# Graph attention over 2708 nodes: five moves in the order of the work (M's block sums, additions of h, sort, W_v's differences, table entries)

## The chip, the cores and the metric

The kernel runs on one core of a Trainium2 chip. A core has TensorE (PE, matrix products; PEld is its loading of weights), VectorE (DVE), ScalarE (ACT), GpSimd (POOL) and SyncE (SP). DMAs are issued from the queues of SP, ACT and POOL. The metric is device microseconds (us) of one execution, as a median of several runs; one execution is also recorded by the profiler, and its trace is what the views below come from.

## The reference

One layer of masked attention over a graph, with a layer norm ahead, in float32. There are N = 2708 nodes of D = 1024 features; the adjacency matrix `adj` holds ones with a chance of 0.00148 each, so about four in a row.

```python
h = jnp.maximum(_layernorm(x, axis=-1), 0.0)
q = h @ W_q.T + b_q
k = h @ W_k.T + b_k
v = h @ W_v.T + b_v
z = scale * (q @ k.T)
spare_z = z * adj
spare_z = jnp.where(spare_z == 0.0, -10000.0, spare_z)
attn = softmax(spare_z, axis=1)
x = x + relu(attn @ v)
```

## The kernel before

**What it computes instead.** It never forms the 2708 x 2708 scores. W_q and W_k are multiplied into one matrix M (1024 x 1024), so that a score is the product of a row of h M + b with a neighbour's row of h. The sum over neighbours is taken over rows of h, and W_v is applied once to the result. Only the neighbours' rows are gathered.

**Rows and tiles.** Nodes stand in 22 tiles (21 of 128 rows and one of 20). Tiles 0 to 11 (`EARLY` = 12) are the early part, the others the late part; each part is sorted by degree, so that all rows of a sorted tile t have at most K[t] neighbours.

**The stages.**

1. *M* (lines 340 to 486, PE's `ps_x`, `ps_y`, `ps_z`). M is formed in four blocks by seven block products, each a sum over `term` calls. `joined` adds a bank into M on DVE. Beside it the statistics of x (`stats`, `root`, `apply`), the stores of h (`keep`) and the searches of adj (`edges`) run, in an order written out as text: `follow("e7 e8")` searches tiles 7 and 8; the letters are s (statistics), m (moments), r (root), a (apply), h (keep), e (edges).
2. *Queries* (units "q"). A unit is a pair of tiles. Its 256 x 1024 by 1024 x 1024 product is done with seven block products (`multiply`, PE's `ps` and `psy`), which need sums of M's blocks (`ts_of_m`, tile T, in `wlow`) and sums of the rows' blocks (`blocks`: `s1` to `s4`). ACT and DVE take the results (`c11`, `c12`, `c21`, `c22`). Units 0 to 5 (`FIRST` = 6) are tiles 0 to 11 in their natural order; later units work on sorted tiles, whose rows are gathered. The searches go on beside units 0 to 2 (`steps_at`).
3. *Sort* (`sort`, line 533). Counts and ranks by two products on PE (`ps_in`, `ps_all`, from `hot`), then the place of each node (`pos_i`). `put` stores the entries of the table (18 words for each node: neighbours, node number, degree) into DRAM at these places by indirect DMAs from POOL, and loads them back sorted (`ptab`).
4. *Attention* (`attention`, `scores`, `weights`, `sums`), a generator that DVE works through: for each sorted tile and slot a neighbour's rows (g) are gathered, multiplied with the query rows (pq, gathered for early tiles, loaded for late ones), exponentiated, and summed into u. `advance` takes steps of it between the products of units from `FIRST` on, `share` of time for each product.
5. *Outputs* (units "o"): pairs of u, again by seven products with W_v, whose blocks' differences (`ts_of_wv`) were stored to `tv_dram`; then x is added and the rows are scattered to the output. The last tile is done alone.

**What sets the order.** PE, SP and, after a point, the rest are ordered by a scheduler. In the stages up to the sort ACT, DVE and POOL run in the order of the program text (`manual_schedule`: `ordered` for ACT and DVE, `pooled` for POOL, closed in `after` at (3, 2)); DVE is in the order of the text again from unit 6 on. `tc.issue_after` holds an instruction behind another in the order of issue. In `after(i)`, line 1068, n is the unit and i the product behind which a step stands. Each engine works its queue in order, so a wait at its head holds all that stand behind it.

**The places the change touches.** `keep` (248): for each tile, a store of h from POOL's queue and an addition into `hsum` on POOL. The order of e7, e8 and the sums `ts_of_m(0, 0)` and `ts_of_m(1, 0, 1, 2, 3)` on DVE, and the product of the bias (`ps_v`, 479), whose halves are subtracted on DVE (483). The loads of W_k's first 128 rows from ACT's queue (348). `put` (511) and the end of `sort` (570). `ts_of_wv` (659): 16 subtractions and 16 stores. `after` (1068): where sort, the differences and the first step of `advance` stand. The index `half_i` (1147) is computed on DVE from the late part of the sorted table.

Of the kernel before, what the change touches and what calls it, by code (L numbers as in the profile page):

```python
# [18 lines left out]
P = 128  # L19
NB = 512  # L20
# [10 lines left out]
EARLY = 12  # L31
# [26 lines left out]
def tile_preln_masked_attention(  # L58
# [12 lines left out]
    nc = tc.nc  # L71
    N, D = x.shape
# [4 lines left out]
    NT = len(tiles)  # L77
# [10 lines left out]
    wk_rows = wk.rearrange("o p c w -> o (p c w)")  # L88
# [29 lines left out]
    hsum = const.tile([P, D], FT, name="hsum")  # L118
# [36 lines left out]
    t = 0  # L155
    while t < NT:
# [4 lines left out]
        t = e  # L161
# [83 lines left out]
                n = tiles[group[i]][1]  # L245
                nc.scalar.activation(xs[i][:n], xs[i][:n], AF.Relu, bias=r[:n, 4, i:i + 1], scale=r[:n, 3, i:i + 1])

    def keep(first):

        group, xs, r = normed.pop(first)  # L250
        for t, xt in zip(group, xs):
            t0, n = tiles[t]
            nc.gpsimd.dma_start(h_dram[t0:t0 + n, :], xt[:n])
            nc.gpsimd.tensor_add(hsum[:n], hsum[:n], xt[:n])  # L254

    normed, adj_loads, kept = {}, [], {}

    def follow(steps):

        for step in steps.split():  # L260
            first, *only = step[1:].split(".")
            first, *last = first.split("-")
            first = int(first)
            if step[0] == "s":
                stats(range(first, int(last[0]) + 1))
            elif step[0] == "m":
                moments(first)
            elif step[0] == "r":
                root(first)
            elif step[0] == "a":  # L270
                apply(first, *[range(int(o[0]), int(o[-1]) + 1) for o in only])
            elif step[0] == "h":
                keep(first)
            else:
                adj_loads.append(edges(first))

# [55 lines left out]
    def ts_of_m(part, *which):  # L332
        cut = slice(part * (P // NH), (part + 1) * (P // NH))
        m = [[M[:, i, j].rearrange("p c (b w) -> p (c b) w", w=P)[:, :, cut] for j in range(2)] for i in range(2)]
        t = [T[:, k].rearrange("p c (b w) -> p (c b) w", w=P)[:, :, cut] for k in range(4)]
        for k in which:
            a, b = ((m[0][1], m[0][0]), (m[1][1], t[0]), (m[1][1], m[0][1]), (m[1][0], t[1]))[k]
            nc.vector.tensor_sub(t[k], a, b)

    with tc.tile_pool(name="w", bufs=1, side="left") as wp:  # L340
# [3 lines left out]
        wk_sb = [wlow[:, H + o] for o in range(H)] + [wp.tile([P, D], FT, name=f"wk{o}") for o in range(H, DC)]  # L344
        for o in range(DC):
            nc.sync.dma_start(wq_sb[o], wq_rows[o * P:(o + 1) * P, :])
            for part in (slice(0, NB), slice(NB, D)) if o == 0 else (slice(0, D),):
                (nc.scalar if o < 2 else nc.sync).dma_start(wk_sb[o][:, part], wk_rows[o * P:(o + 1) * P, part])

        t1 = [work.tile([P, D], FT, tag="hT", name=f"t1_{k}", bufs=2) for k in range(2)]  # L350

# [109 lines left out]
        for i in range(H):  # L461
            term(Y[i], i, (0, 1), lambda o: b_half(o, 1))
            joined(Y[i], 1, 1, i)
            if i == 1:
                follow("a20 e4 a0 m2 m3")
        follow("e5 r2 h20 h0")
        for i in range(H):
            term(Z[i], i, (1, 0), lambda o: b_half(o + H, 1))
            joined(Z[i], 0, 1, i)
            if i == 0:  # L470
                follow("a2 e6")
        follow("e7 e8")
        ts_of_m(0, 0)
        ts_of_m(1, 0, 1, 2, 3)
        for i in range(H):
            if i == 2:
                for half in range(NH):
                    ps = psum.tile([P, NB], FT, tag="acc", name="ps_v")
                    nc.tensor.matmul(ps, ones, acc_b[:, half * NB:(half + 1) * NB], start=True, stop=True)
                    pw = P // NH  # L480
                    nc.scalar.copy(bp_sb.rearrange("q (c p) -> q c p", c=DC)[:, :, half * pw:(half + 1) * pw],
                                   ps.rearrange("q (p c) -> q c p", c=DC))
                nc.vector.tensor_sub(bp_sb[:, NB:], bp_sb[:, NB:], bp_sb[:, :NB])
            term(Y[i], i, (1, 1), lambda o: b_half(o + H, 0))
            evicted(Y[i], 1, 0, i)
# [13 lines left out]
    FIRST = EARLY // 2  # L499

    def first_rows(n):

        rows_of[FIRST + n] = [row_tile(f"qr_{t}") for t in (EARLY + 2 * n, EARLY + 2 * n + 1)]
        for k, row in enumerate(rows_of[FIRST + n]):
            last = gather(row, h_dram[:, :], EARLY + 2 * n + k, SLOTS, P)
        return last
# [1 line left out]
    def tiles_of(lo, hi):  # L508
        return list(enumerate(tiles))[lo:hi]

    def put(lo, hi):

        puts = []
        for t, (t0, n) in tiles_of(lo, hi):
            put = nc.gpsimd.indirect_dma_start(  # L515
                out=tab_dram[:, :], out_offset=bass.IndirectOffsetOnAxis(ap=pos_i[:n, t:t + 1], axis=0),
                in_=tab[:n, t, :], in_offset=None)
            for other in puts:
                tc.declare_no_dep(put.ins, other.ins, reason="rows of a permutation")
            puts.append(put)  # L520
        full = min(hi, FULL)
        loads = [nc.gpsimd.dma_start(ptab[:, lo:full, :],
                                     tab_dram[lo * P:full * P, :].rearrange("(t p) w -> p t w", p=P))]
        if hi > FULL:
            loads.append(nc.gpsimd.dma_start(ptab[:REST, FULL, :], tab_dram[FULL * P:, :]))
        for load in loads:
            for put in puts:
                tc.add_manual_dep(load.ins, put.ins.name,
                                  mybir.DependencyInfo(mybir.DependencyClass.Sync, mybir.DependencyReason.DATA),
                                  reason="every row of the part")  # L530
        return loads[-1]

    def sort():
# [33 lines left out]
                                    AX.X, ALU.add)  # L567
        placed = nc.vector.tensor_copy(pos_i, deg)

        put(EARLY, NT)  # L570
        with tc.issue_after(first_rows(0).ins):
            loaded = put(0, EARLY)
        with tc.issue_after(loaded.ins):
            first_rows(1)
        return placed

# [41 lines left out]
    def natural_rows(n):  # L618
# [5 lines left out]
    ops_of[0][2]()  # L624
    banks_of = {0: banks_for(bp_sb)}
    ts_of_m(0, 1, 3, 2)
    follow("h2")
    natural_rows(1)
    ps = psum.tile([P, NB], FT, tag="tp", name="ps_b")
    nc.tensor.matmul(ps[:, 0:3], ones, part, start=True, stop=True)  # L630
# [3 lines left out]
    nc.vector.tensor_scalar(large[:, 0:1], large[:, 0:1], 10000.0, None, op0=ALU.is_gt)  # L634
    nc.vector.tensor_scalar(large[:, 1:2], large[:, 1:2], 250000.0 / D, None, op0=ALU.is_gt)

    steps_at = {(0, 0): "s4-5 e9", (0, 1): "r4 e10", (0, 3): "e11 a4", (0, 5): "h4 s6-7 e12", (0, 6): "r6 e13",
                (1, 0): "a6 h6", (1, 1): "e14", (1, 3): "s8-9", (1, 5): "r8 e15", (1, 6): "e16 a8 h8",
                (2, 0): "s10-11", (2, 1): "e17 r10", (2, 3): "e18", (2, 5): "a10 h10 e19", (2, 6): "e20 e21"}

# [15 lines left out]
        assert len(adj_loads) == NT  # L656
        free.extend(slots + [M.rearrange("p i j (a c) w -> p i j a (c w)", a=2)[:, 0, 1, a, :] for a in range(2)])

    def ts_of_wv():
        with tc.issue_after(placed[0].ins):  # L660
            for c in range(4):
                b11, b12 = slots[2 * c][:, :NB], slots[2 * c][:, NB:]
                b22, b21 = slots[2 * c + 1][:, :NB], slots[2 * c + 1][:, NB:]
                nc.vector.tensor_sub(b11, b12, b11)
                nc.vector.tensor_sub(b12, b22, b12)
                nc.vector.tensor_sub(b22, b22, b11)
                nc.vector.tensor_sub(b21, b21, b22)
                for k, r in enumerate((b11, b22, b12, b21)):
                    nc.sync.dma_start(tv_dram[k][:, c, :], r)
# [387 lines left out]
    for n, unit in enumerate(units):  # L1057
# [8 lines left out]
        results = (q_results if kind == "q" else o_results)(ta, tb)  # L1066

        def after(i):
            if (n, i) == (3, 2):
                pooled.close()  # L1070
                with tc.issue_after(products[-1].ins):
                    placed.append(sort())
                ordered.close()
                ts_of_wv()
            if n == FIRST - 1 and i == 5:

                chain.append(behind[-1])
                next(stream)
            if n == FIRST - 1 and i == 6:
                chain.append(behind[-1])  # L1080
            if (n, i) >= (FIRST, 0):
                advance(share)
            if nxt is not None:

# [272 lines left out]
```

## Time and profile before

| | us |
|---|---|
| median of 3 runs (lowest, highest) | 680.77 (679.22, 680.97) |
| the profiled execution | 680.76 |
| its span, first to last instruction | 679.0 |
| PE, DVE, POOL, ACT busy | 655.5, 525.7, 410.6, 263.5 |
| mean granted clock of PE | 0.994 |
| DMA | 190.62 MB, mean 281 GB/s |

The span is 1.76 us shorter than the profiled execution's time. A row of the timeline has the start in us, the duration in us, the engine, the line of the kernel, the operation, output<-inputs, the shape, the count, and in brackets the idle time of the engine ahead of it with what ended it. A wait "A <- B: total, times, longest" says that A waited for B. Several instructions of one kind are merged in one row ("x2"); a "product" of a block on PE is 8 rows' worth (four matmuls in float32, two instructions each). Durations of PE are modelled at their ends.

### The profile page before, as it was taken

The page shows a single profiled execution, that of the slowest core. Times are in us where ns is not written, and L with a number is a line of the kernel's source. Part 1 is how long each engine was busy: PE and PEld are TensorE (multiplying, and loading weights), DVE is VectorE, ACT ScalarE, POOL GpSimd, SP SyncE. Part 2 cuts the span into 40 slices and gives each one's busy share as a digit, 9 for nine tenths or more (in the row PEclk, how much of TensorE's full clock was granted, in tenths as well). Part 3 has the DMA queues.
Part 4 walks back from the last instruction along what each step waited for, and adds up shares of the span by engine and source line. Part 5 has one row for each costly group of instructions (what it writes and reads, how often), then busy time and mean ns, then how long its engine had stood idle before and what let it go on. Part 6 is the DMA issues. An engine that isn't in the chain of part 4 may idle for free.

```text
span 679.0 us, 6344 instructions
## 1 busy us (share of the span) xinstructions
PE 655.5 (97%) x1764; PEld 332.9 (49%) x1764; DVE 525.7 (77%) x1002; ACT 263.5 (39%) x396; POOL 410.6 (60%) x396
## 2 busy tenths in 40 slices
PE   7999997999998999999999999999999999999995
PEld 4777764444444444434444444444444444444442
DVE  5999859997798422099989859898999989989301
ACT  3466965755762212123322212233432333322220
POOL 2549995166453666476765437676776787883342
PEclk9999999999999999999999999999999999999998
DMA  8997889598767934789997999989998889696653
GB/s 342 408 357 248 317 299 407 198 322 344 284 225 237 297 104 127 256 273 367 370 334 263 411 417 401 295 235 313 279 286 266 256 267 338 187 263 217 152 151 120
DMA packets 61588, 190.62 MB, mean 281 GB/s; under 512 B 9753, under 2 KB 10105, under 8 KB 60650
## 3 DMA queue, kind: packets, MB, share of 16 engines
q0 software_dynamic: 34176, 107.67, 48.9%
q1 hardware_dynamic: 26362, 79.32, 31.7%
q10 hardware_dynamic: 1008, 3.15, 1.3%
q8 instruction: 16, 0.26, 0.2%
q14 instruction: 26, 0.21, 0.1%
HBM read 159.81 MB, written 43.88 MB: 300 GB/s over the span
## 4 chain that ended last, share of the span: by engine, by line
PE 52%; DVE 16%; issue 12%; DMA 10%; POOL 5%; ACT 2%; POOLq 0%; ACTq 0%; DVEq 0%
PE ps L840 19%; PE psy L840 14%; PE ps_y L368 6%; DVE u L777 5%; PE ps_x L368 5%; PE ps_z L368 4%; DMA u_dram<-u 3%; DVE junk L724 3%; DMA y<-in_x_dram,tab 3%; POOL g L494 2%; PE pt L311 2%; PE lone_q L1033 2%; DVE s L590 2%; DMA g<-h_dram,tab 2%; DVE at L292 2%
## 5 line engine op out<-in xcount | busy, mean ns | idle before, releaser
L494 POOL DMA_INDIRECT g<-h_dram,tab x107 | 133.1, 1244 | 62.7 <-issue 23.0
L840 PE MATMUL ps<-M,a 128*128 128x512 f32 x320 | 144.3, 593 | 0.1
L840 PE MATMUL psy<-wlow,s 128*128 128x512 f32 x320 | 144.1, 592 | 0.0
L724 DVE SCALAR_TENSOR_TENSOR junk<-g,pq 128x1024 uint8<-128x1024 f32 x95 | 116.3, 1224 | 22.7 <-DMA pq<-q_dram,tab 15.5
L777 DVE SCALAR_TENSOR_TENSOR u<-g,coef,u 128x1024 f32<-128x1024 f32 x78 | 100.1, 1283 | 7.4 <-ACT u L769 4.3
L840 PEld LDWEIGHTS ps<-M,a 128*128 128x128 f32 x320 | 59.4, 190 | 68.2 <-issue 67.4
L840 PEld LDWEIGHTS psy<-wlow,s 128*128 128x128 f32 x320 | 59.2, 190 | 66.5 <-issue 66.5
L840 PE MATMUL psy<-wlow,a 128*128 128x512 f32 x160 | 72.6, 596 | 5.7 <-DVE q L906 3.6
L840 PE MATMUL ps<-wlow,s 128*128 128x512 f32 x160 | 73.7, 604 | 3.5 <-ACT part L631 3.5
L292 DVE FIND_INDEX8 at<-ones,adj 128x8 uint32<-128x685 f32 (+1 forms) x88 | 74.4, 865 | 0.0
L840 PE MATMUL ps<-M,s 128*128 128x512 f32 x160 | 72.1, 592 | 0.0
L930 POOL DMA_INDIRECT y<-in_x_dram,tab x21 | 36.9, 1755 | 36.4 <-DMA tail_dram<-y 11.4
L285 ACT ACTIVATE sized<-adj 128x2708 uint8<-128x2708 f32 (+1 forms) x22 | 54.2, 2465 | 6.5 <-DMA adj<-in_adj_dram 5.4
L254 POOL TENSOR_TENSOR hsum<-hsum,x 128x1024 f32<-128x1024 f32 (+1 forms) x22 | 52.5, 2387 | 0.5
L840 PEld LDWEIGHTS psy<-wlow,a 128*128 128x128 f32 x160 | 29.8, 190 | 45.5 <-issue 34.4
L840 PEld LDWEIGHTS ps<-wlow,s 128*128 128x128 f32 x160 | 30.9, 194 | 43.2 <-issue 38.3
L840 PEld LDWEIGHTS ps<-M,s 128*128 128x128 f32 x160 | 30.2, 190 | 36.8 <-issue 36.4
L590 DVE TENSOR_TENSOR s<-a,pt 128x512 f32<-128x512 f32 x40 | 25.7, 681 | 15.2 <-ACT a L586 15.2
L769 ACT ACTIVATE u<-g,coef 128x1024 f32<-128x1024 f32 x16 | 18.4, 1149 | 46.6 <-DVE coef L768 46.6
L586 ACT COPY a<-pt 128x512 f32<-128x512 f32 x60 | 33.1, 591 | 7.3 <-PE pt L311 7.3
L678 POOL DMA_INDIRECT out_dram<-y,tab x21 | 30.3, 1442 | 8.9 <-issue 5.8
L515 POOL DMA_INDIRECT tab_dram<-tab,pos_i x22 | 24.1, 1094 | 8.3 <-issue 6.1
(234 smaller groups left out, 864.0 us busy)
## 6 DMA issues: line engine op xcount, KB each, us to landing
adj<-in_adj_dram SPq DMA_DIRECT2D x21, 1354.0 KB, 12.0
x<-in_x_dram SPq DMA_DIRECT2D x21, 512.0 KB, 10.9
h_dram<-x POOLq DMA_DIRECT2D x21, 512.0 KB, 6.3
u_dram<-u POOLq DMA_DIRECT2D x12, 512.0 KB, 6.2
or<-u_dram SPq DMA_DIRECT2D x12, 512.0 KB, 8.6
pq<-q_late POOLq DMA_DIRECT2D x9, 512.0 KB, 6.7
g<-in_wv_dram SPq DMA_DIRECT2D x16, 256.0 KB, 5.8
tv_dram<-g SPq DMA_DIRECT2D x16, 256.0 KB, 4.9
```

The lines of the kernel that those rows point to most:

```text
L254: nc.gpsimd.tensor_add(hsum[:n], hsum[:n], xt[:n])
L285: nc.scalar.activation(sized[:n], a[:n, :, :PW], AF.Abs, accum_out=total[:n, t:t + 1])
L292: nc.vector.max_index(at[:n, t - first_t, g, :], ones[:n, 0:8], a[:n, g, :])
L368: mm = nc.tensor.matmul(bank, a_tile(o + H * a[0], a[1], i), b(o), start=first and o == 0, stop=(o == H - 1), skip_group_check=True)
L494: return nc.gpsimd.indirect_dma_start(out=dst, out_offset=None, in_=src, in_offset=off, bounds_check=N - 1, oob_is_err=False)
L586: nc.scalar.copy(ops[name], bank)
L590: step = (eng or nc.vector).tensor_tensor(ops[name], a, b, op=op)
L678: to = nc.gpsimd.indirect_dma_start(out=out, out_offset=bass.IndirectOffsetOnAxis(ap=ptab.bitcast(U32)[:n, t, SLOTS:SLOTS + 1], axis=0), i ...
L724: chained(lambda: nc.vector.scalar_tensor_tensor(junk, g_of[t][s], 1.0, tq[t], op0=ALU.mult, op1=ALU.mult, accum_out=zall[:, t, s:s + 1]))
L777: chained(lambda: nc.vector.scalar_tensor_tensor(u, g_of[t][s], coef[:, at[t][s]:at[t][s] + 1], u, op0=ALU.mult, op1=ALU.add))
L840: mm = nc.tensor.matmul(bank, a[:, c, :], b[:, c, :], start=False, stop=(c == 3), skip_group_check=True)
L930: return nc.gpsimd.indirect_dma_start(out=y[:n], out_offset=None, in_=x, in_offset=off, compute_op=ALU.add)
```

## The change

- The sums of M's blocks that the first units need stand ahead of the searches e7 and e8 on DVE, not behind them; the bias product stands one step sooner.
- The additions of h's tiles 0 to 3 into `hsum` are parted from the stores (step "k" stores alone) and done in units 0's first two steps (step "+").
- W_k's first half row-block is loaded as before; its second half is loaded behind the second row-block.
- Sort stands behind product 3 of unit 3, not behind product 2; W_v's differences are asked for in two parts, behind products 1 and 2 of unit 4, and ordered behind the last of q's additions, not behind `pos_i`.
- `put` is parted into `put` (stores of entries) and `reload`. Order before: late entries, load of the late table, gather of unit 6's rows, early entries, load of the early table, gather of unit 7's rows. Order after: late entries, half of the early entries, load of the late table, the other early entries, gather of unit 6's rows, load of the early table, gather of unit 7's rows.
- `advance` begins one product later, at (6, 1).

```diff
-    def keep(first):
+    def keep(first, add=True):
...
             nc.gpsimd.dma_start(h_dram[t0:t0 + n, :], xt[:n])
-            nc.gpsimd.tensor_add(hsum[:n], hsum[:n], xt[:n])
+            if add:
+                nc.gpsimd.tensor_add(hsum[:n], hsum[:n], xt[:n])
+            else:
+                owed[t] = xt
+    owed = {}
+    def owe(t):
+        xt = owed.pop(t)
+        nc.gpsimd.tensor_add(hsum, hsum, xt)
...
-            for part in (slice(0, NB), slice(NB, D)) if o == 0 else (slice(0, D),):
-                (nc.scalar if o < 2 else nc.sync).dma_start(wk_sb[o][:, part], wk_rows[o * P:(o + 1) * P, part])
+            part = slice(0, NB) if o == 0 else slice(0, D)
+            (nc.scalar if o < 2 else nc.sync).dma_start(wk_sb[o][:, part], wk_rows[o * P:(o + 1) * P, part])
+            if o == 1:
+                nc.scalar.dma_start(wk_sb[0][:, NB:], wk_rows[:P, NB:])
...
-        follow("e5 r2 h20 h0")
+        follow("e5 r2 h20 k0")
...
-        follow("e7 e8")
         ts_of_m(0, 0)
         ts_of_m(1, 0, 1, 2, 3)
+        follow("e7 e8")
         for i in range(H):
-            if i == 2:
+            if i == 1:
...
-        put(EARLY, NT)
-        with tc.issue_after(first_rows(0).ins):
-            loaded = put(0, EARLY)
-        with tc.issue_after(loaded.ins):
+        late, early = [], []
+        put(EARLY, NT, late)
+        with tc.issue_after(late[-1].ins):
+            put(0, EARLY // 2, early)
+        with tc.issue_after(early[-1].ins):
+            back = reload(EARLY, NT, late)
+        with tc.issue_after(back.ins):
+            put(EARLY // 2, EARLY, early)
+        with tc.issue_after(early[-1].ins):
+            rows = first_rows(0)
+        with tc.issue_after(rows.ins):
+            back = reload(0, EARLY, early)
+        with tc.issue_after(back.ins):
             first_rows(1)
...
-    follow("h2")
+    follow("k2")
...
-    steps_at = {(0, 0): "s4-5 e9", (0, 1): "r4 e10", (0, 3): "e11 a4", (0, 5): "h4 s6-7 e12", (0, 6): "r6 e13",
+    steps_at = {(0, 0): "s4-5 e9 +0 +1", (0, 1): "r4 e10 +2 +3", (0, 3): "e11 a4", (0, 5): "h4 s6-7 e12", (0, 6): "r6 e13",
...
-    def ts_of_wv():
-        with tc.issue_after(placed[0].ins):
-            for c in range(4):
+    def ts_of_wv(lo, hi):
+        with tc.issue_after(behind[-1].ins):
+            for c in range(lo, hi):
...
-            if (n, i) == (3, 2):
+            if (n, i) == (3, 3):
                 pooled.close()
                 with tc.issue_after(products[-1].ins):
                     placed.append(sort())
                 ordered.close()
-                ts_of_wv()
+            if (n, i) in ((4, 1), (4, 2)):
+                ts_of_wv(2 * i - 2, 2 * i)
...
-            if (n, i) >= (FIRST, 0):
+            if (n, i) >= (FIRST, 1):
                 advance(share)
```

The order on each engine, as both programs are built, differs by this, by two row gathers (unit 8's) that stand ahead of the first q gathers on POOL's queue, and by the places of single steps of the attention between the products of later units.

More of the change, by code (lines that the diff above doesn't have):

```diff
@@ L271, in follow @@
                 apply(first, *[range(int(o[0]), int(o[-1]) + 1) for o in only])
-            elif step[0] == "h":
-                keep(first)
+            elif step[0] in "hk":
+                keep(first, step[0] == "h")
+            elif step[0] == "+":
+                owe(first)
             else:
@@ L509, in tiles_of, with put @@
         return list(enumerate(tiles))[lo:hi]
-    def put(lo, hi):
-        puts = []
+    def put(lo, hi, puts):
         for t, (t0, n) in tiles_of(lo, hi):
@@ L520, in put, with reload @@
             puts.append(put)
+    def reload(lo, hi, puts):
         full = min(hi, FULL)
```

## The prediction

> **What bounds the kernel now.** I read the page first, for the busy shares:
>
> ```profile
> PE 655.5 (97%) x1764; PEld 332.9 (49%) x1764; DVE 525.7 (77%) x1002; ACT 263.5 (39%) x396; POOL 410.6 (60%) x396
> ```
>
> TensorE (PE) is busy 655.5 of 679.0 us, and the change takes no product away. So it can only win back the 23.5 us in which PE stands, or lose there. Some 8.5 us of them lie behind the last product (at 670.5). The waits of PE name the rest (total, times, longest):
>
> ```profile
> PE psy L840 <- DVE q L906: 3.6, 2, 2.0
> PE ps L840 <- ACT part L631: 3.5, 1, 3.5
> PE ps_y L403 <- POOL hsum L119: 2.8, 1, 2.8
> PE psy L840 <- DVE p L940: 2.1, 3, 1.2
> PE ps_in L554 <- DVE hot L550: 2.1, 1, 2.1
> ```
>
> The timeline of PE tells where (start, duration, wait ahead in brackets):
>
> ```profile
> 116.50 5.37 PE L840 MATMUL ps<-wlow,s 128*128 128x512 f32 x8 [3.50 <-ACT part L631]
> ...
> 210.09 0.90 PE L554 MATMUL ps_in<-hot,before 128*128 128x396 f32 x2 [2.06 <-DVE hot L550]
> ...
> 228.68 3.70 PE L840 MATMUL psy<-wlow,a 128*128 128x512 f32 x8 [1.54 <-DVE q L906]
> ...
> 305.93 3.70 PE L840 MATMUL psy<-wlow,a 128*128 128x512 f32 x8 [2.02 <-DVE q L906]
> ```
>
> All four end on VectorE (DVE; the first by ACT's copy of what DVE wrote). Eight such rows take 3.43 us in the chain of waits; after the 3.50 us wait they take 5.37, with the granted clock at 0.67 in 116 to 120 us: 1.94 us more. After 2.06 and 2.02 us the clock stays 1.00.
>
> From 287.57, the first score, DVE is the second bound: 9.7 to 9.9 of each 10 us until 350. The chain of waits runs over DVE, gathers and POOL from 368 to 583, then over PE to the end. A gain ahead of 287 counts only if the attention work starts earlier too. It starts on a gather of stored q rows (issued 283.19), which waits for products of unit 5: PE's gain moves it.
>
> **Sums ahead of the searches (e7, e8).** DVE has 23.15 us between the last joined add (91.92) and the subtraction of bp_sb (115.07), on which PE waits. The rows of that stretch, POOL's and then DVE's:
>
> ```profile
> 104.80 2.36 POOL L254 TENSOR_TENSOR hsum<-hsum,x 128x1024 f32<-128x1024 f32 x1
> ...
> 107.71 2.76 POOL L254 TENSOR_TENSOR hsum<-hsum,x 128x1024 f32<-128x1024 f32 x1
> ```
>
> ```profile
> 104.99 6.57 DVE L338 TENSOR_TENSOR wlow<-M 128x1024 f32<-128x1024 f32 x2
> 111.66 1.23 DVE L338 TENSOR_TENSOR wlow<-M,wlow 128x1024 f32<-128x1024 f32 x1
> ...
> 115.07 0.69 DVE L483 TENSOR_TENSOR bp_sb<-bp_sb 128x512 f32<-128x512 f32 x1
> ```
>
> Two subtractions beside POOL's additions take 6.57 us instead of 2.3: each stands until an addition ends. Searches in the same stretch (0.87 us each) are not slowed. Work: e7 6.6, e8 3.4, five subtractions at a pitch of 1.14, 5.7: together 15.7. The 2.97 us in which DVE waits for e8's rows (there at 101.6) go away. New order: subtractions from 92.0, beside POOL's additions of tiles 20 and 21 (93.2 to 98.4) and, sooner than before, of 0 and 1 right behind four stores. Each engine in turn, I get: the third and fourth subtraction wait 2.4 each, 4.8; the additions of 0 and 1 run from 102.5 to 107.2 and stop e7's tensor_tensor for 1.4. End: 91.92 + 15.7 + 6.2 = 113.8, 1.3 earlier. Bounds: no collision, 107.6 (7.4 earlier); all four additions in the way (9.6), 117.2 (2.1 later). I take the middle, since three collisions follow from the issue times.
>
> PE's wait becomes 2.2, near the two that cost no clock, so the 1.94 go too: 3.2. But unit 1's first product needs s1 (138.90 to 139.54 in DVE's rows) at 140.13: 0.6 of slack, and DVE works without a break from 115 to 153. So 1.3 + 0.6 = **1.9 won** (bounds: 5.4 won, that is 3.50 + 1.94; 2.1 lost).
>
> **Additions of h later.** Four of 2.37 us leave 99 to 110.5; two run at 102 to 107 (counted above), two behind root's steps of tile 4 at about 126. There DVE searches, which POOL does not slow. 0; if they hit one tensor_tensor, 2.4 lost on DVE (the 128x128 one at 192.85 takes 2.81 instead of 0.29). The four stores of h are issued up to 7 us earlier; e10's and e11's rows are asked for up to 9 us later (their buffers are e7's and e8's), at 106 and 114, with 12.0 median to landing, needed at 127 and 130: covered, by 4 us at the tighter.
>
> **W_k's half later.** It goes behind a 512 KB load, 1.3 us at the 400 GB/s of that stretch. DVE's run that starts with it (10.25) has its last result that PE needs next at 34.15, needed at 36.27: 2.1 hide it. 0 (bounds 0 and, without the cover, 1.3 lost).
>
> **Sort one product later.** DVE now does two block additions (1.3) ahead of sort, whose first seven steps end 2.3 after the last search: hot at 207.4 + 1.3 + 2.3 = 211.1 on the old clock. PE meanwhile has eight transposes (0.87) and the rest of the product (1.7) in front: ready at 210.5. The wait falls from 2.06 to 0.6: **1.5 won** (bounds 2.06 and 0).
>
> **W_v's differences.** Now 16 subtractions stand right behind pos_i (218.3 to 227.9), and q's addition (L906) behind them: the 1.54 us wait. The changed order has that addition ahead of pos_i and the 16 still right behind it, in spite of the two parts: **1.5 won** (bounds 1.54; 0 if pos_i then waits for PE). Total so far 4.9.
>
> **Table interleaved.** Entries stored and the table's consumer on DVE:
>
> ```profile
> 227.37 1.50 POOL L515 DMA_INDIRECT tab_dram<-tab,pos_i  x1 [0.30 <-issue]
> 229.17 0.97 POOL L515 DMA_INDIRECT tab_dram<-tab,pos_i  x1 [0.30 <-issue]
> ```
>
> ```profile
> 243.34 0.21 DVE L1147 TENSOR_SCALAR half_i<-tab 128x1 uint32<-128x1 uint32 x2 [14.71 <-DMA tab<-tab_dram]
> ```
>
> Beside DVE's 16 subtractions six stores go at a pitch of 1.79, then at 1.28. Now ten stores, 6.1 us of POOL standing until they land, and the late table's load (239.96). After: pos_i some 2.7 earlier, sixteen stores (6 x 1.79 + 10 x 1.28 = 23.5 from 216.0), load at 239.5, landed 3.4 later: 242.9. half_i waits for it, and behind half_i on DVE stand unit 5's s1 to s4 and unit 4's two additions. s1 would be there at 243.7; PE needs it at 248.55 - 4.9 = 243.7. So 0, with nothing in reserve: each us that the load comes later costs one (bounds 0; 5.1 lost at 1.79 for all sixteen). [...] The first unit's rows are gathered at 249, 5 later, landed 6.1 later, transposed at 262.44 - 4.9 = 257.5: covered. The early table comes some 8 sooner, and nothing waits for it.
>
> **Attention one product later.** Two row gathers move ahead of the q gather on POOL, into 7.4 us in which it stood. To the end of the addition PE waits for (305.88), DVE has 18.3 us from 287.57; two of the attention steps now stand behind it, so 15.9: done at 298.6, PE there at 299.0. The 2.02 go. But DVE is full, so PE is then 2.0 ahead of it and later waits (0.61, 0.32, 1.21) can give it back: I take **1.0 won** (bounds 4.1 won, all of both; 3.4 lost, one product).
>
> Sum 1.9 + 1.5 + 1.5 + 1.0 = 5.9. The profiled execution took 680.76 us (679.0 span and 1.76 around), the median is 680.77: 680.8 - 5.9 = **674.9 us**.
>
> **The rivals.** (a) No collision on the sums: 5.4 instead of 1.9, 671.4; with all of the last part 668.3. For it: DVE issues its five back to back. Against: the 6.57. (b) All four collide: 2.1 lost instead of 1.9 won, 678.9. (c) The table's load is late, all stores at 1.79: 5.1 lost, 680.0. For it: no reserve. Against: the slow rows end with the 16 subtractions. (d) The other side: the attention work sets the end and starts late. The two row gathers bring 1 MB, 2.8 us at the 374 GB/s of 276 to 280, in front of the last q stores; the units' gain stops at gathers in the full stretch from 370 to 430 (DMA share 1.02 and more); and the stream stays one product, 3.43, behind. 680.8 + 3.4 = 684.2. It decides once the first score comes no earlier than 287.6. Against: in the stretch from 350 to 390 DVE waits 5.5 us for PE, so an earlier PE helps it.
>
> **How the numbers follow.** Forecast 0.50, (a) 0.13, (b) 0.12, (c) 0.08, (d) 0.17. The range of 670 to 682 leaves out half of (d) and the far end of (a). The likeliest case's own is 672 to 678. A measurement here tells 0.3%, 2.0 us: faster is below 678.7. Forecast and (a) lie there, and half of (b): 0.69. Same: half of (b) and (c), 0.14. Slower: (d), 0.17.
>
> **What would show it.** Right: PE's wait ahead of unit 0's second product about 2, with no fall of the clock; no wait on q's addition at 224; sort's wait below 1; half_i within 1 us of 243; first score near 282.7; the wait at 305.93 gone. Wrong: subtractions of M's blocks with several of 3 us or more; half_i beyond 245; PE's waits on L906's or L940's successor above 5 us between 300 and 583.

## The result and the profile after

| | before | after |
|---|---|---|
| median of 7 runs (lowest, highest), us | 680.71 (679.22, 680.97) | 676.45 (675.16, 679.82) |
| the profiled execution, us | 680.76 | 675.16 |
| its span, us | 679.0 | 673.5 |
| PE, DVE, POOL, ACT busy, us | 655.5, 525.7, 410.6, 263.5 | 652.8, 524.4, 414.3, 264.7 |

The changed kernel takes 0.9948 of the time before, with a 95% interval of 0.9927 to 0.9969: faster by 4.3 us in the median. The forecast was 674.9. The profiled execution is the fastest of the seven. The waits of PE in the changed kernel (total, times, longest):

```profile
PE ps_y L417 <- POOL hsum L119: 2.8, 1, 2.8
PE pt L323 <- ACT M L396: 2.7, 2, 1.9
PE ps_in L570 <- DVE hot L566: 1.6, 1, 1.6
PE pt L323 <- DVE u L802: 1.6, 1, 1.6
PE ps L865 <- DVE s L615: 1.5, 1, 1.5
```

The 3.50 us for the bias and the 3.6 us for q's additions are gone. Three things stand in their place: 2.7 us for ACT's M, 1.5 us for a sum `s`, and 1.6 us for u (of the 2.1 us for p, 0.4 is left). The timeline of PE tells where the waits ahead of the attention stage lie (start, duration, wait in brackets):

```profile
106.89 0.66 PE L323 MATMUL pt<-ident,x 128*128 128x128 f32 x4 [1.87 <-ACT M L396]
108.35 1.63 PE L323 MATMUL pt<-ident,x 128*128 128x128 f32 x12 [0.81 <-ACT M L396]
...
114.81 3.60 PE L865 MATMUL ps<-wlow,s 128*128 128x512 f32 x8
...
208.80 0.90 PE L570 MATMUL ps_in<-hot,before 128*128 128x396 f32 x2 [1.64 <-DVE hot L566]
...
244.55 3.67 PE L865 MATMUL ps<-wlow,s 128*128 128x512 f32 x8 [1.53 <-DVE s L615]
...
299.82 3.60 PE L865 MATMUL psy<-wlow,a 128*128 128x512 f32 x8
```

Unit 0's second product (114.81) no longer waits and takes 3.60, not 5.37, at a granted clock of 1.00 from 112 to 120. The product that waited 2.02 at 305.93 starts at 299.82 without a wait. New are the wait ahead of the transposes of unit 0, and one of 1.53 behind the late table.

The starts of the same products in the two profiles say where the 5.6 us between the profiled executions came from:

| stretch, from the start of one product to that of the next | before | after | won |
|---|---|---|---|
| to M's second row of blocks (`ps_x<-wk,wq`) | 22.38 | 20.73 | 1.65 |
| to unit 1's first product on `wlow` | 117.59 | 115.77 | 1.82 |
| to unit 4's product on block a12 | 94.84 | 92.62 | 2.22 |
| to the product that waited for q's addition in unit 6 | 71.12 | 70.70 | 0.42 |
| to the first product of the last tile (656.60, 651.09) | 350.67 | 351.27 | -0.60 |

The first row turns out not to belong to the change (next section). The other four make 3.9 us. No run parts the bias product's place or sort's place from the rest of the change; what is said of them below is worked out from the rows.

### The profile page after: what moved, and what is told of

It reads as the page before. It is cut to its first block, busy times and chain, and to the rows that moved or that the text cites. A ratio compares the mean times of both kernels' runs of the same rounds, so it can differ in the third digit from the quotient of the medians.

```text
span 673.5 us, 6358 instructions
## 1 busy us (share of the span) xinstructions
PE 652.8 (97%) x1764; PEld 332.1 (49%) x1764; DVE 524.4 (78%) x1002; ACT 264.7 (39%) x396; POOL 414.3 (62%) x396
## 4 chain that ended last, share of the span: by engine, by line
PE 54%; DVE 20%; POOL 10%; issue 8%; DMA 5%; ACT 3%; ACTq 0%; POOLq 0%; DVEq 0%
PE ps L865 28%; PE psy L865 20%; DVE u L802 3%; PE pt L323 3%; DVE at L304 3%; POOL hsum L255 3%; DVE junk L749 3%; POOL tab_dram L528 2%; PE lone_q L1058 2%; DMA g<-h_dram,tab 2%; DVE acc_b L438 1%; DVE st L210 1%; DMA wlow<-in_wk_dram 1%; DVE s L615 1%; POOL g L508 1%
## 5 line engine op out<-in xcount | busy, mean ns | idle before, releaser
L749 DVE SCALAR_TENSOR_TENSOR junk<-g,pq 128x1024 uint8<-128x1024 f32 x95 | 116.3, 1225 | 21.0 <-DMA pq<-q_dram,tab 15.3
L865 PE MATMUL ps<-wlow,s 128*128 128x512 f32 x160 | 72.0, 593 | 1.5 <-DVE s L615 1.5
L255 POOL TENSOR_TENSOR hsum<-hsum,x 128x1024 f32<-128x1024 f32 (+1 forms) x18 | 42.7, 2370 | 0.4
L878 ACT COPY psy<-ps 128x512 f32<-128x512 f32 x20 | 11.5, 573 | 62.2 <-PE ps L865 49.1
L703 POOL DMA_INDIRECT out_dram<-y,tab x21 | 28.8, 1373 | 8.8 <-issue 5.8
```

The costliest lines, as they stand in the source:

```text
L703: to = nc.gpsimd.indirect_dma_start(out=out, out_offset=bass.IndirectOffsetOnAxis(ap=ptab.bitcast(U32)[:n, t, SLOTS:SLOTS + 1], axis=0), i ...
L749: chained(lambda: nc.vector.scalar_tensor_tensor(junk, g_of[t][s], 1.0, tq[t], op0=ALU.mult, op1=ALU.mult, accum_out=zall[:, t, s:s + 1]))
L865: mm = nc.tensor.matmul(bank, a[:, c, :], b[:, c, :], start=False, stop=(c == 3), skip_group_check=True)
```

## The experiments

All times are medians beside runs of the kernel before on the same chip (680.3 to 680.6 there). "Sums" are the five subtractions of M's blocks on DVE, "additions" the four additions of h's tiles 0 to 3 on POOL.

**Undo W_k's order** (`e_wk`).

```diff
-            part = slice(0, NB) if o == 0 else slice(0, D)
-            (nc.scalar if o < 2 else nc.sync).dma_start(wk_sb[o][:, part], wk_rows[o * P:(o + 1) * P, part])
-            if o == 1:
-                nc.scalar.dma_start(wk_sb[0][:, NB:], wk_rows[:P, NB:])
+            for part in (slice(0, NB), slice(NB, D)) if o == 0 else (slice(0, D),):
+                (nc.scalar if o < 2 else nc.sync).dma_start(wk_sb[o][:, part], wk_rows[o * P:(o + 1) * P, part])
```

> The changed kernel with W_k's loads alone as before the change: both halves of the first 128 rows, then the second 128 rows. In the profile of the changed kernel the first product of M's second row (ps_x<-wk,wq, line 382) starts 1.65 us earlier than before the change (20.73 against 22.38), and that lead stays on every later product. Theory (the order of W_k's loads sets it): the start goes back to about 22.4, the time rises by about 1.6 us over the changed kernel's (median 676.45, profiled 675.16). Rival (the first products' speed differs from one execution to the next whatever the order of loads): the start may lie anywhere from 20.7 to 22.4 and the median moves by less than 0.7.

677.46 us (675.79 to 677.81), ratio 0.9952 (0.9935 to 0.9968); the second row of blocks started at 20.98, not at 22.4. So the order of the loads did not set the 1.65. Over all profiles of this study that start lies at 20.98, 20.98, 21.09 and 22.38 with the old order and anywhere from 20.73 to 22.28 with the new one: it differs from execution to execution. The 1.0 us that this median is above the changed kernel's lies within both spreads.

**Undo the sums' place** (`e_nosums`).

```diff
+        follow("e7 e8")
         ts_of_m(0, 0)
         ts_of_m(1, 0, 1, 2, 3)
-        follow("e7 e8")
```

> The changed kernel with the searches of tiles 7 and 8 ahead of the sums of M's blocks again (DVE's order alone changes, the additions of h stay late). Theory of the prediction: the sums' place won 1.9 (the wait of PE ahead of unit 0's second product, 3.50, and 1.94 of lower clock behind it), so +1.9 us over the changed kernel, with the wait back at line 865's first product on ps and no wait of PE on ACT's M at 107. Rival 1: the late additions of h alone free DVE (the two subtractions that took 6.57 beside POOL's additions stand alone now), so the wait ahead of the second product stays below 2 and the time within 0.7. Rival 2: the wait at 107 (1.87 + 0.81, transposes behind ACT's M) also goes away, and this order is up to 1 us faster.

674.94 us (673.98 to 676.45), ratio 0.9922 (0.9904 to 0.9939): 1.5 us below the changed kernel, where the prediction's theory wanted 1.9 above. Neither the 3.50 nor the 2.7 us wait is in its trace. On DVE, the subtractions:

```profile
101.68 0.09 DVE L304 MATCH_VALUE_LOAD at<-ones,adj 128x8 f32 x1 [3.19 <-DMA adj<-in_adj_dram]
...
105.06 2.41 DVE L350 TENSOR_TENSOR wlow<-M 128x1024 f32<-128x1024 f32 x2
107.58 1.23 DVE L350 TENSOR_TENSOR wlow<-M,wlow 128x1024 f32<-128x1024 f32 x1
```

The two that took 6.57 us before the change take 2.41, although they stand in the old place: POOL's late additions have left the stretch. Rival 2 of the expectation is the nearest.

**The additions alone** (`b_adds`), in the kernel before: the "k" and "+" steps of the diff, and nothing else.

> The kernel before the change with only the additions of h's tiles 0 to 3 parted from the stores and done in unit 0's first two steps; the sums of M's blocks stay behind the searches e7 and e8. Theory now (the additions of h, not the sums' place, are what freed the stretch ahead of unit 0's second product): the two subtractions that took 6.57 beside them take 2.4, PE's wait of 3.50 with its 1.94 of lower clock falls below 0.5, and unit 1's first wlow product then waits for s1 by up to 1; the stretch to unit 1's wlow product gets 3 to 4.5 us shorter. The time falls by 3 to 4, unless the later waits (hot 2.06, q's additions 1.54 and 2.02) grow: at least 2. The theory of the prediction (the additions cost and give 0, the sums' place gives all): within 0.7 of before.

676.51 us (675.54 to 677.79), ratio 0.9944 (0.9928 to 0.9960). This one part is worth 3.9 us, nearly as much as the whole change (4.3).

**The sums alone** (`b_sums`), in the kernel before.

```diff
-        follow("e7 e8")
         ts_of_m(0, 0)
         ts_of_m(1, 0, 1, 2, 3)
+        follow("e7 e8")
```

> The kernel before the change with only the sums of M's blocks ahead of the searches e7 and e8; the additions of h stay with their stores. The term of the prediction (1.9 won by this move, with the additions of h costing and giving nothing) would make it 678.8. Theory now (the additions of h are the cause of the 3.50 us wait; the sums moved ahead only change which of DVE's and POOL's instructions collide, either DVE's subtractions at 3.4 each or POOL's root of tile 2 at 1.0 a step, by the phase of the execution): 0 to 1 below before, 679.5 to 680.5, with the wait of PE ahead of unit 0's second product or at the transposes of 107 still 2 to 4 in all. Together with the additions alone (676.51) this parts the two.

679.23 us (677.50 to 682.41 in 12 runs), ratio 0.9992 (0.9978 to 1.0007): no change that can be told. The 1.9 us of the prediction would be a ratio of 0.9972, outside this interval. The twelve runs lie in two groups, seven from 677.50 to 679.41 and five from 681.14 to 682.41, and the profiled one is the fastest of them. Its trace has the wait ahead of the transposes, 2.6 us in two, where the 3.50 was.

Why the early place costs is seen on three engines of the changed kernel. DVE runs the subtractions back to back, at 1.2 us each:

```profile
90.27 2.39 DVE L350 TENSOR_TENSOR wlow<-M 128x1024 f32<-128x1024 f32 x2
92.77 1.22 DVE L350 TENSOR_TENSOR wlow<-M,wlow 128x1024 f32<-128x1024 f32 x1
```

POOL, meanwhile, is in the root of tile 2, small steps that take 0.19 to 0.20 each at tile 4 (the same lines, 121.31 to 122.34), where no subtraction runs:

```profile
90.25 0.20 POOL L232 TENSOR_TENSOR r<-r 128x2 f32<-128x2 f32 x1
90.53 1.05 POOL L233 TENSOR_TENSOR r<-r 128x2 f32<-128x2 f32 x1
91.67 1.04 POOL L234 TENSOR_SCALAR r<-r 128x2 f32<-128x2 f32 x1
92.79 1.25 POOL L235 TENSOR_TENSOR r<-r 128x2 f32<-128x2 f32 x1
```

and ACT waits for that root, then applies it, then sizes three tiles of adj, and only then evicts M for PE's transposes:

```profile
96.35 2.38 ACT L246 ACTIVATE x<-x,r 128x1024 f32<-128x1024 f32 x2 [6.79 <-POOL r L237]
...
106.25 0.58 ACT L396 ACTIVATE M<-ps_y 128x512 f32<-128x512 f32 x1
```

From 90.53 on, each of POOL's steps took 1.02 to 1.25 us, and DVE's subtractions kept their 1.2. The same order of instructions also came out the other way: in `e_half`, below, the sums came 1.4 us later and two of them stood beside POOL's additions instead, 3.38 each. On DVE there:

```profile
91.68 2.35 DVE L350 TENSOR_TENSOR wlow<-M 128x1024 f32<-128x1024 f32 x2
94.14 1.23 DVE L350 TENSOR_TENSOR wlow<-M,wlow 128x1024 f32<-128x1024 f32 x1
95.28 3.38 DVE L350 TENSOR_TENSOR wlow<-M 128x1024 f32<-128x1024 f32 x1
98.58 3.38 DVE L350 TENSOR_TENSOR wlow<-M,wlow 128x1024 f32<-128x1024 f32 x1
```

**ACT's applies behind the sizing** (`e_a2`).

```diff
             if i == 0:
-                follow("a2 e6")
+                follow("e6")
...
-        follow("e7 e8")
+        follow("e7 a2 e8")
```

> The changed kernel with one step of ACT moved: the applies of tile a2 stand behind the searches' sized e6 and e7, not ahead of e6. In the changed kernel ACT stands 6.79 us for POOL's root of tile 2 (held from 92.5 to 96.3 beside DVE's subtractions), and the evictions of M that PE's transposes wait for (1.87 + 0.81 at 107 to 109) stand behind it. Theory: both waits go or fall below 0.5, product a starts about 2.5 earlier than 111.27, and the time falls by 0.6 to 2.5 us (unit 1's first product then waits for s1 on DVE, which bounds the gain). Rival: the transposes are then held by other evictions, or DVE's bp_sb (108.23 to 109.66) is what counts: within 0.5 us.

677.58 us (673.25 to 677.90), ratio 0.9937 (0.9915 to 0.9959). The waits at the transposes fell from 2.68 to 1.17, but PE then waited 1.51 for the bias and 1.20 for unit 1's `s`: DVE bounds the stage, as the rival has it. (The median is 1.1 above the changed kernel's, more than the rival's 0.5, but its runs spread over more than 4.) Here a subtraction took 3.38 and tile 7's two search steps 3.46 and 2.39 beside POOL.

**half_i out of the way** (`e_half`).

```diff
-    for h in range(NH):
-        nc.vector.tensor_scalar(half_i[:, h:h + 1], ...)
+    with tc.issue_after(chain[-1].ins):
+        for h in range(NH):
+            nc.vector.tensor_scalar(half_i[:, h:h + 1], ...)
```

> The changed kernel with the two instructions of half_i moved on DVE behind the searches' and blocks' chain, so that unit 5's sums s1 to s4 no longer stand behind the late table's load. Theory: half_i (done at 243.8, waiting 18.54 for the table) is all that holds s1, so PE's wait of 1.53 at 244.55 goes, and the products to 283 come 1.5 earlier; the first q gather too. End: -1.5 us if the attention stage keeps it, -0.5 if DVE, full from 283 to 350, gives it back in later waits. Rival: s1 also waits for something else (ACT's or PE's results of unit 4), or the first gather of pq or of g, which half_i feeds, comes later: 0 or slower.

676.29 us (674.84 to 676.54), ratio 0.9935 (0.9919 to 0.9951). The wait at unit 5 is gone; PE waits 0.42 for the rows of unit 6 instead. In its profile the sort's product came 2.07 later than in the changed kernel's and the end of the span 0.9 later, so about 1.1 were won in between and kept. The median does not show it. The M stage could hide it, since it differs by 2.0 us between the profiles of the four kernels that have this order (table below), but only one execution of this kernel has a profile.

**Both, with the sums behind** (`n_half`).

> The changed kernel with the sums of M's blocks behind the searches e7 and e8 again and half_i's two instructions behind the chain of additions. Both alone: sums behind gave 674.94 with a wait of 1.47 for s1 at unit 5 behind half_i; half_i moved took that wait away and brought one of 0.42 on the gathered rows of unit 6. Theory: the two add up, 1.1 below 674.94, about 673.8. Rival: the attention work, bound by the store and gather of q, does not start earlier, and DVE's later waits take it: 674.9.

675.28 us (672.83 to 677.02), ratio 0.9916 (0.9894 to 0.9937). The unit 5 wait is gone, a collision ahead of it hides the gain in the profiled execution (below). The median is above both figures and the spread covers both, so the runs cannot decide between 673.8 and 674.9.

**The table's order as before** (`n_table`, sums behind): late entries, late table, rows of unit 6, early entries, early table.

> The version with the sums of M's blocks behind the searches (674.94), with the order of the table before the change: late entries, late table, rows of unit 6, early entries, early table. Theory (ten stores stand ahead of the late table's load instead of sixteen): the load is issued 3 to 5 us earlier, half_i stands at 238 to 240 instead of 242.7, PE's wait of 1.47 for unit 5's s1 goes, the rows of unit 6 are there sooner; the g gathers come 3 to 4 later (264 instead of 260.4) and are still ahead of the pq gather at 278: 1.5 us faster, about 673.5. Rival (interleaving pays): the first g rows or the rows of units 7 and 8 come too late, and it is 674.9 or slower.

672.67 us (671.99 to 676.29), ratio 0.9902 (0.9879 to 0.9926): 2.3 below the same kernel with the interleaved table. In the changed kernel, POOL waits for the early stores as well before it loads the late table (the first row is the last late store, the second the last early one):

```profile
230.02 0.89 POOL L528 DMA_INDIRECT tab_dram<-tab,pos_i  x1 [0.30 <-issue]
...
237.61 0.97 POOL L528 DMA_INDIRECT tab_dram<-tab,pos_i  x1 [0.30 <-issue]
240.33 1.09 POOL L538 DMA_DIRECT2D tab<-tab_dram  x1 [1.75 <-DMA tab_dram<-tab,pos_i]
```

```profile
243.59 0.21 DVE L1173 TENSOR_SCALAR half_i<-tab 128x1 uint32<-128x1 uint32 x2 [18.54 <-DMA tab<-tab_dram]
```

No store of this trace takes more than 6.4 us to land, so the late ones are there by 236.4: the 1.75 us at 240.33 is for early ones. With the old order, POOL, then DVE:

```profile
228.62 0.89 POOL L528 DMA_INDIRECT tab_dram<-tab,pos_i  x1 [0.30 <-issue]
233.48 1.12 POOL L538 DMA_DIRECT2D tab<-tab_dram  x1 [3.97 <-DMA tab_dram<-tab,pos_i]
```

```profile
236.72 0.21 DVE L1168 TENSOR_SCALAR half_i<-tab 128x1 uint32<-128x1 uint32 x2 [13.07 <-DMA tab<-tab_dram]
```

half_i is there 6.0 us sooner than in the same kernel with the interleaved table (242.72), and unit 5 does not wait. The first score comes at 280.60, against 282.61: the gathers of g, first issued at 261.27, are still ahead of the pq gather at 276.26.

**W_v's differences as before** (`t_wv`, `n_table`'s kernel with the 16 subtractions in one part, behind the places of sort).

> The version with the sums of M's blocks behind the searches and the table's order as before (672.67), with W_v's differences in one part behind the places of sort, as before the change. Theory: the 16 subtractions stand ahead of q's addition on DVE again, PE waits 1.5 at unit 4's fourth product (near 222) and all of it stays to the end: 1.5 to 1.8 slower, 674.2 to 674.5. Rival: since sort stands one product later, the addition comes ahead of them anyway and nothing changes: 672.7.

672.54 us (672.10 to 676.33 in 5 runs), ratio 0.9882 (0.9868 to 0.9897): nothing changes, as the rival said. DVE's order is the same:

```profile
217.55 0.69 DVE L926 TENSOR_TENSOR q<-psy,p 128x512 f32<-128x512 f32 x1
218.15 0.18 DVE L584 CAST pos_i<-deg 128x22 uint32<-128x22 f32 x1
218.23 1.30 DVE L684 TENSOR_TENSOR g<-g 128x512 f32<-128x512 f32 x2
```

So it is not the parting that brings q's addition ahead of `pos_i`. By elimination it is the sort's new place, one product later; no run moves the sort alone.

**advance at the first product again** (`t_adv`, `n_table`'s kernel with `>= (FIRST, 0)`).

> The version with the sums of M's blocks behind the searches and the table's order as before (672.67), with advance beginning at the first product of unit 6 again. Theory: PE's wait for q's addition in unit 6, near 295, returns with 1.8 to 2.1, and PE's waits on u and p later (1.6, 0.4, 0.6) change to the three on p (0.6, 0.3, 1.2), so that 0.8 of it comes back: 1.3 slower, 674.0. Rival 1: all of it stays lost, 2.1 slower, 674.8. Rival 2: DVE, full from 279 to 345, gives all back: 672.7.

675.00 us (673.48 to 679.73 in 9 runs), ratio 0.9931 (0.9909 to 0.9953): 2.3 slower, nearest to rival 1. The wait for q's addition is back on PE, and this time the clock falls with it:

```profile
299.28 5.40 PE L860 MATMUL psy<-wlow,a 128*128 128x512 f32 x8 [2.17 <-DVE q L926]
```

```profile
295.00:299.00 4.00, 2.11 (x5) 0.57 (x3) 3.93 (x12) 1.48 (x2) 3.39 (x3) 1.00 0.94 324
299.00:303.00 4.00, 3.72 (x6) 1.70 (x7) 3.96 (x6) 0.83 (x3) 2.88 (x3) 0.67 0.99 353
```

(The second fence gives busy time of PE, PEld, DVE, ACT and POOL in each stretch, then PE's granted clock, DMA share and GB/s.) From the product at 290 to that at 305 or 310, 15.48 us became 19.61. Of the 4.13, 0.78 came back until 609 or 613, where the waits for p take the place of that for u.

**Sums between the searches** (`n_mid`: `e7`, sums, `e8`, all four additions behind tile 4's root, and half_i moved).

> The changed kernel with the sums of M's blocks between the searches e7 and e8, all four late additions of h behind root's steps of tile 4, and half_i's two instructions put behind the chain of additions. With the sums behind both searches DVE stood 3.19 us for e8's rows of adj, at 98.5 to 101.7, and the subtractions then ran alone, 5.9 us at 105 to 111. Theory: the subtractions fill that stand, nothing of POOL's runs beside them, DVE is done about 3 earlier, so neither PE's transposes (2.7 in the changed kernel) nor unit 1's product (0.94 for s1 with the sums last) wait; with half_i's 1.5 also gone the time is 2 to 3.5 below the 674.94 of the version with the sums behind both searches. Rival: the four additions in one row (9.6 us behind tile 4's root) hold DVE's operations at 124 to 134 or the buffers of h, and give it back: no faster than 674.

674.04 us (671.58 to 677.39), ratio 0.9914 (0.9886 to 0.9941). The mechanism is there in the profiled execution of 672.14: subtractions alone on 98.0 to 103.8, no wait at the transposes, 0.24 for unit 1's `s`. Three of its six executions are slower by about 4, and the median, 0.9 below 674.94, meets the rival's figure and not the theory's 2 to 3.5.

**Sums between, table as before** (`best3`).

```diff
+        follow("e7")
         ts_of_m(0, 0)
         ts_of_m(1, 0, 1, 2, 3)
-        follow("e7 e8")
+        follow("e8")
...
         put(EARLY, NT, late)
-        with tc.issue_after(late[-1].ins):
-            put(0, EARLY // 2, early)
+        reload(EARLY, NT, late)
+        with tc.issue_after(first_rows(0).ins):
+            put(0, EARLY, early)
...
-    steps_at = {(0, 0): "s4-5 e9 +0 +1", (0, 1): "r4 e10 +2 +3", ...
+    steps_at = {(0, 0): "s4-5 e9", (0, 1): "r4 e10 +0 +1 +2 +3", ...
```

> The changed kernel with the sums of M's blocks between the searches e7 and e8, the four late additions of h behind the root of tile 4, and the table's order as before the change. Theory: it has the shorter M stage of the first (unit 1's product waits 0.2 for s1 instead of 1.15, and nothing runs on POOL beside the subtractions) and the earlier table of the second (no wait at unit 5): 1 below 672.67, about 671.7, and its executions lie closer together, since a collision of a search's step with POOL's additions of tiles 20 and 21 is the only one left. Rival: the executions 4 us apart stay (671.6 to 677.4 with the sums between, 672.0 to 676.3 with the sums behind), since it is the additions of tiles 20 and 21 that make them: median between 672 and 674.

671.68 us (671.23 to 671.76 in 4 runs), ratio 0.9868 (0.9854 to 0.9882): the fastest here, 4.8 below the changed kernel and 8.7 below the one before. All waits of PE above 0.2 us that are left in it:

```profile
PE ps_y L417 <- POOL hsum L119: 2.8, 1, 2.8
PE ps_in L571 <- DVE hot L567: 1.7, 1, 1.7
PE pt L323 <- DVE u L798: 1.6, 1, 1.6
PE ps_x L382 <- DMA wlow<-in_wk_dram: 0.9, 1, 0.9
PE psy L861 <- ACT psy L874: 0.6, 1, 0.6
PE psy L861 <- DVE p L961: 0.4, 1, 0.4
```

Four runs do not show that its executions always lie so close: `n_mid` has the same M stage and did not.

**What splits the executions.** The time from M's second row of blocks to unit 1's first product on `wlow` takes the start's spread out of the comparison:

| kernel | us |
|---|---|
| before | 117.6 |
| sums alone ahead (b_sums) | 115.8 |
| sums ahead, additions late (after, e_half, e_a2, e_wk) | 115.8, 116.3, 117.4, 117.8 |
| additions late, sums behind (b_adds, e_nosums, n_table, t_adv) | 113.9, 113.4, 113.5, 113.4 |
| the same, with a collision (n_half, t_wv) | 117.5, 117.5 |
| sums between (n_mid, best3) | 112.6, 112.4 |

In `t_wv` the two small steps of tile 7's search met POOL's additions of tiles 21 and 0, where in `n_table`, with the same order, they slipped in between two additions. `t_wv`, DVE and POOL, then `n_table`, DVE:

```profile
95.85 2.42 DVE L309 TENSOR_TENSOR cand<-first,at 128x128 f32<-128x128 f32 x1
98.31 4.45 DVE L310 SCALAR_TENSOR_TENSOR cand<-at,cand 128x128 f32<-128x128 uint32 x1
```

```profile
95.75 2.37 POOL L255 TENSOR_TENSOR hsum<-hsum,x 20x1024 f32<-20x1024 f32 x1
98.05 2.17 POOL L253 DMA_DIRECT2D h_dram<-x  x4
100.23 4.81 POOL L264 TENSOR_TENSOR hsum<-hsum,x 128x1024 f32<-128x1024 f32 x2
```

```profile
94.56 0.48 DVE L309 TENSOR_TENSOR cand<-first,at 128x128 f32<-128x128 f32 x1
95.07 0.29 DVE L310 SCALAR_TENSOR_TENSOR cand<-at,cand 128x128 f32<-128x128 uint32 x1
```

The second step stood from 98.31 on, though an addition ran beside it only from 100.23; why it did not finish beside the four stores is not shown. 1.3 us later at the first step cost 6.1 us more on DVE, a PE wait of 3.44 and 1.8 of lower clock (0.58 in 116 to 120). It would account for the two groups of `t_wv` (four runs at 672.1 to 672.6, the profiled one at 676.33). That the same splits `n_table` (672.0 to 672.7 and 676.1 to 676.3) and `n_mid` fits, but their slower executions have no profile.

## Why the prediction was right, and where it was not

The time, 1.6 us above the forecast, and the sign were right. Against the 5.9 of the sum stand 4.3 in the medians, and 3.9 in the profiled execution without its start. Point by point:

- **Sums and additions together**: 1.9 forecast, 1.8 measured in the profiles. That the two figures are so close is luck, since the split failed. The text gave all of it to the sums' place and put "0" on the additions of h. Run apart, the additions are worth 3.9 and the sums' place 0 to 1.1 alone, and 1.5 lost on top of the additions. The step that failed is the cost of the additions' leaving: the 6.57 row was read as something that the subtractions had to flee from, when the additions beside them left by the same change. Of the three collisions that were forecast on DVE, the two on subtractions of M's blocks did not come in the profile. A step of tile 7's search stood 2.1 (2.37 instead of 0.29 at 100.00). DVE reached the subtraction of bp_sb at 108.23 (109.9 without the start), not at 113.8. The mechanism was also seen from one side only. I counted what POOL's additions do to DVE's subtractions (2.4 each; `e_half` shows 3.38 instead of 1.2) and not what the subtractions do to POOL's root (1.02 to 1.25 a step instead of 0.19 to 0.23) and, through ACT, to PE's transposes.
- **W_k's half later**: 0, and nothing measured to the contrary. The start's spread was not foreseen.
- **Sort one product later**: its wait was to fall from 2.06 to 0.6 and fell to 1.64, so 0.4 instead of 1.5. DVE's and POOL's rows show the missing 1.1: the first step of sort took 1.02 instead of 0.34, and its copy 0.60 instead of 0.19, beside POOL's sums of unit 4. DVE before, then DVE and POOL after:

```profile
207.64 0.34 DVE L539 TENSOR_SCALAR sort<-keys 128x352 f32<-128x352 f32 x1
...
208.58 0.19 DVE L541 COPY tab<-deg 128x22 f32<-128x22 f32 x1
```

```profile
205.26 1.02 DVE L555 TENSOR_SCALAR sort<-keys 128x352 f32<-128x352 f32 x1
...
206.87 0.60 DVE L557 COPY tab<-deg 128x22 f32<-128x22 f32 x1
```

```profile
204.81 1.27 POOL L615 TENSOR_TENSOR s<-s,a 128x512 f32<-128x512 f32 x1 [2.22 <-DVE s L615]
206.16 1.27 POOL L615 TENSOR_TENSOR s<-a,s 128x512 f32<-128x512 f32 x1
```

- **W_v's differences**: 1.5 forecast and 1.8 measured in that stretch (the wait of 1.54 is gone), with the wrong name on it. `t_wv` shows that the parting does nothing; by elimination the sort's place moves q's addition. Sort and W_v together were 3.0 forecast, 2.2 measured.
- **Table interleaved**: 0 forecast "with nothing in reserve". The load went out at 240.33 instead of 239.5, because it waited 1.75 for the early stores too, which the sum had left out, and half_i began at 243.59, 0.7 later than forecast; PE was there 0.7 earlier. All of these hold the 1.65 of the start: without it half_i would be 2.3 later than forecast and PE 1.0, since the sort gave less than forecast (`pos_i` 1.3 earlier than before instead of 2.7). So 1.5 was lost in the profile (2.3 between the medians of `e_nosums` and `n_table`). The direction of the bound was right; a term with no reserve should not have been priced at its best end.
- **Attention one product later**: 1.0 forecast, 1.4 in the profiles (2.02 gone, 0.60 given back). With the table as before, undoing it cost 2.3, since its wait also took the clock down (0.67 in 299 to 303). That part of the price was not in the sum. The first score came at 283.48 (forecast near 282.7) and q's addition at 298.20 (forecast 298.6).

So the sum was 2.0 too high in the profiles: 1.5 on the table, 0.8 on sort and W_v together and 0.1 on sums and additions, less 0.4 on the attention.

Of the prediction's own signs, the wait of about 2 ahead of unit 0's second product did not come (none there, 2.68 ahead of the transposes), and sort's wait did not fall below 1. The others came: half_i near 243, the first score near 282.7, and no wait left for q's additions. Two readings were off and change little: PE needs unit 1's s1 at 139.97, where its row begins, not at 140.13, so the slack was 0.4 and not 0.6; and of the 5.5 us that DVE waits "for PE" from 350 to 390, 3.9 are for ACT's copies.

Of the rivals, (c), a late table, came in part: 1.5 of its 5.1. Of (a), no collision, the cause came and the gain did not: DVE's subtractions took 1.2 each, but POOL's root stood instead, and PE waited at the transposes. (d), a late stream, did not come: the first score was 4.1 us earlier than before.

The interval of `e_nosums` overlaps those of `n_table` and the changed kernel, and `t_adv`'s overlaps `n_table`'s. The steps of 1.5, 2.3 and 2.3 between them rest on medians of six to nine runs and on the traces, which show the place of each.

## What to carry to other kernels

When one change moves both sides of a collision, price each side alone, in both directions: which engine stood changed here with a shift of 1.4 us (the changed kernel and `e_half`), and 1.3 us later at one small step cost the stretch 4 (`n_table` and `t_wv`). Move the work that nobody waits for (here, additions into a sum needed much later) before moving the work that PE waits for. And a step that arrives exactly when it is needed is to be priced as a loss (here 1.5 of a bound of 5.1), not as zero.

## What the runs showed of the hardware

- **The granted clock behind a stand of PE did not go by the stand's length alone.** Stands of 2.06 (before) and 1.64 (after) left it at 1.00. One of 2.17 brought it to 0.67 in the next 4 us (`t_adv`), one of 2.59 to 0.57 (`n_half`, 5.25 us for 3.43 of work). Two short ones, 1.87 and 0.81, left it at 1.00 from 104 to 112 in the changed kernel; 1.83 and 0.80 at the same place in `e_wk` brought 0.50 in 108 to 112 and 0.68 in 112 to 116. What else decides it is not shown.
- **Two operations with one input stood beside POOL too**: sort's tensor_scalar took 1.02 instead of 0.34 and its copy 0.60 instead of 0.19, both beside POOL's sums (1.27 each). The tensor_reduce between the two, beside the same sums, took 0.52 as before, and the searches' passes over adj (find_index8, 0.85 to 0.89 each) are not slowed in any stretch read here. No run takes POOL's sums away.
- **The first block product of M took 15.45 to 16.94 us** for the same 32 rows (the profiles after and before), at a granted clock of 1.00 in both from 5 to 21 us, with DMA at 1.02 to 1.04 of its share; why is open.
